# A graph network's message stage: from the scheduler's order to one fixed order of half-quad steps

## The chip, the cores and the metric

The kernel runs on one core of a Trainium2 chip. The metric is device time in microseconds (us). Before the change the median of 3 runs is 2623.31 us (2615.97 to 2633.4).

Engines are named as in the profile: PE (matrix multiply; PEld is its weight load), DVE (vector), ACT (activation), POOL (here almost only the issue of gathers), SP (here the issue of plain DMAs). L734 is line 734 of the kernel before the change.

## What is computed

A graph of 3125 nodes with 96 features and 100000 edges, sorted by destination, goes through four residual blocks: a ten-hop propagation, a softmax-weighted aggregation (layer 1), an edge-conditioned message block, and two graph convolutions. Each block gets the layer-normalised, rectified features. The change concerns the third block, whose core in the reference is:

```python
def _mlp(h, W, b, gamma, beta):
    h = jax.nn.relu(h @ W + b)
    mu = jnp.mean(h, axis=0)
    var = jnp.mean(jnp.square(h - mu), axis=0)
    return gamma * (h - mu) * jax.lax.rsqrt(var + EPS) + beta
node_feat = _mlp(x, W_node, b_node, g_node, beta_node)
edge_feat = _mlp(edge_attr, W_edge, b_edge, g_edge, beta_edge)
row, col = (edge_index[0], edge_index[1])
message = jnp.concatenate([x[row], x[col], edge_feat], axis=1)
message = _mlp(message, W_msg, b_msg, g_msg, beta_msg)
agg = jax.ops.segment_sum(message, col, num_segments=node_feat.shape[0])
return agg + node_feat
```

`row` is the source of an edge, `col` its destination.

## The kernel before

The kernel is written tile by tile in a framework that tracks the data dependencies, sets all semaphores, gives out buffers from pools (`bufs=n` buffers of one name in rotation), and orders the instructions of each engine by a planner of its own. So the program text of a loop is not the order in which an engine gets its instructions. Each engine then works strictly through its list.

Edges and nodes are first turned into count matrices (the first 400 us or so); ten hops of matrix products follow (`gather`, L372 to L384), then layer 1 (L574 to L654), which walks over 25 blocks of 128 nodes. For each block, layer 1 also writes two tables to DRAM: `Pt` (the source part of the message product) and `Qt` (the destination part), as pairs of fp16 halves, high and low (L637 to L644). Pools opened by then: `up` with two large fp16 tiles `u`, `mid`, and `late` (L532), whose tiles live until the end.

The message stage (L658 to L778) takes the edges in 98 quads of 1024 edges; a quad has two halves of 4 x 128 edges. The destinations of a quad lie within 128 consecutive nodes from the quad's first destination on. At its head the stage fetches three index lists from DRAM (`rlT`, `srow`, `rows`, L661 to L666) and builds a comparison pattern `li` on POOL (L667, L668). Then, for each quad:

- SP reads the quad's first node from `rows` into a register (L712) and loads `qg` (128 rows of `Qt`, L715), `et` (edge attributes, three buffers, L720) and `rlb` (destinations relative to the first, spread over 128 partitions, L722; four buffers in the space of `h`).
- DVE turns the destinations into two one-hot matrices: `ohT` (L724) and `oh` (L726).

and for each half:

- POOL gathers the source rows of `Pt`, one indirect DMA for each 128 edges, four in all (L733 to L735), into one of six buffers `pgs` that lie in a `u` tile.
- PE multiplies the edge attributes (`ef`, L737); ACT rectifies them to fp16 `eh` (L739), DVE takes the remainder `el` (L741).
- PE sums four products for each 128 edges into `pre` (PSUM, two buffers): with `ohT` and `qg` (L745), with `eh` (L746), with `el` (L747), and the gathered rows through the identity (L748).
- ACT copies the low part (`mt`, L750), DVE adds the high part (L751) and takes the maximum with 0 less the estimate `cb` of the mean (`m`, L753). ACT and DVE split `m` into an fp16 pair (L761, by L369 and L370) in one of four buffers `mms`, which also lie in a `u` tile and are listed in the profile as `u`.
- PE adds the pair to the quad's sums by `oh` (`segs`, L766) and to the Gram matrix (`gram`, L768).

At the end of a quad, PE adds what the last quad had for this quad's first node (`carry`, L765); ACT and DVE make `sacc` from `segs` (L771, L772), and SP stores it to `Sd` (L773). From the fifth quad on one of 15 pieces of the node branch is done per quad (`node_piece`, L687 to L708; its PSUM tile shares the two `ef` buffers). In the last half DVE clears the 352 edges that do not exist (L759).

After the stage `gs` is read from `gram` (L778), five small weights are loaded (L781 to L783), and the last two layers begin with the load of `Sd` (L793) and two tiles `u` from the pool `l3` (L790).

Of the kernel before, what the change touches and what calls it, by code (L numbers as in the profile page):

```python
# [9 lines left out]
F32 = mybir.dt.float32  # L10
F16 = mybir.dt.float16
I32 = mybir.dt.int32
F8 = mybir.dt.float8e4
U8 = mybir.dt.uint8
AF = mybir.ActivationFunctionType
ALU = mybir.AluOpType
# [4 lines left out]
P = 128  # L21
N, D, E = 3125, 96, 100000
NB = 25
NP = NB * P
EP, EC = 125, 800
GC = 8
# [3 lines left out]
HC = 4  # L30
# [10 lines left out]
Q, QE = 98, 1024  # L41
# [13 lines left out]
def narrow(ctx: ExitStack, tc: tile.TileContext, a: dict, out: bass.AP, flag: bass.AP):  # L55


    nc = tc.nc
# [33 lines left out]
    where = [const]  # L92
# [252 lines left out]
    def over_b(t, nb=NB):  # L345

        return t[:, None, :].to_broadcast([P, nb, D])
# [19 lines left out]
    def split(hi, lo, t):  # L367

        S.activation(hi, t, AF.Copy)  # L369
        V.tensor_sub(lo, t, hi)  # L370
# [200 lines left out]
    V.memset(hT[0][D:, :], 1.0)  # L571
    cb = where[-1].tile([P, D], F32, name="cb")

    with tc.tile_pool(name="l1", bufs=1) as lp, tc.tile_pool(name="l1w", bufs=3) as wp, \  # L574
            tc.tile_pool(name="l1p", bufs=3, space=PSUM) as pp, tc.tile_pool(name="l1q", bufs=1, space=PSUM) as qp:
        ps = qp.tile([P, 2, D], F32, name="pq")
# [81 lines left out]
    with tc.tile_pool(name="msg", bufs=1) as lp, tc.tile_pool(name="gath", bufs=6) as gp, \  # L658
            tc.tile_pool(name="msgw", bufs=3) as wp, tc.tile_pool(name="msgs", bufs=1, space=PSUM) as p1, \
            tc.tile_pool(name="msgp", bufs=2, space=PSUM) as p2:  # L660
        rlT = lp.tile([P, Q * 8], F16, name="rlT2")  # L661
        nc.sync.dma_start(rlT, rlT_d)
        srow = lp.tile([P, Q * 8], I32, name="srow")
        nc.sync.dma_start(srow, srcT_d)
        rows = lp.tile([1, Q], I32, name="rows")
        nc.sync.dma_start(rows, row_d)  # L666
        li = lp.tile([P, P, 4], F16, name="li2")  # L667
        G.iota(li, pattern=[[1, P], [0, 4]], base=0, channel_multiplier=0, allow_small_or_imprecise_dtypes=True)  # L668

        t = up.tile([P, NB, 2 * D + 2], F16, name="u").rearrange("p b d -> p (b d)")  # L670
        mms = [t[:, i * HC * GM:(i + 1) * HC * GM].rearrange("p (c d) -> p c d", c=HC) for i in range(4)]
# [35 lines left out]
                    T.transpose(ps[:, s, :], rT[:, c0 + s * P:c0 + (s + 1) * P], ident[:D, :D])  # L707
                V.tensor_add(x[:, b0:b0 + nb, :], x[:, b0:b0 + nb, :], ps)  # L708

        acc = None  # L710
        for g in range(Q):
            r0 = nc.values_load(rows[0:1, g:g + 1], engines=(mybir.EngineType.SP,), min_val=0, max_val=N - 1,  # L712
                                skip_runtime_bounds_check_because="a dst is a node")
            qg = gp.tile([P, 2 * D], F16, name="qg")
            nc.sync.dma_start(qg, Qt[bass.ds(r0, P), :])  # L715
            et = wp.tile([18, QE], F16, name="et")
            n = min(QE, E - g * QE)
            if n < QE:
                V.memset(et, 0.0)
            nc.sync.dma_start(et[:, :n], ea_d[:, g * QE:g * QE + n])  # L720
            rlb = rlbs[g % len(rlbs)]
            nc.sync.dma_start(rlb, bass.AP(tensor=rl_d.tensor, offset=rl_d.offset + g * QE, ap=[[0, P], [1, QE]]))  # L722
            ohT = wp.tile([P, QE], F16, name="ohT")
            V.tensor_scalar(ohT, rlb, part, None, ALU.is_equal)  # L724
            oh = wp.tile([P, 2, P, 4], F16, name="oh")
            V.tensor_tensor(oh, li[:, None, :, :].to_broadcast([P, 2, P, 4]),  # L726
                            rlT[:, g * 8:g * 8 + 8].rearrange("p (s c) -> p s c", s=2)[:, :, None, :].to_broadcast(
                                [P, 2, P, 4]), ALU.is_equal)
            seg = segs[:, g % 2, :GM]
            for half in range(GC // HC):  # L730
                k0 = g * GC + half * HC
                pg = pgs[(g * (GC // HC) + half) % len(pgs)]
                for c in range(HC):  # L733
                    G.indirect_dma_start(out=pg[:, c, :], out_offset=None, in_=Pt,  # L734
                                         in_offset=bass.IndirectOffsetOnAxis(ap=srow[:, k0 + c:k0 + c + 1], axis=0))  # L735
                ps = p2.tile([P, 512], F32, name="ef")[:D, :]
                T.matmul(ps, We, et[:, half * HC * P:(half + 1) * HC * P], start=True, stop=True)  # L737
                eh = wp.tile([D, HC * P], F16, name="eh")
                S.activation(eh, ps, AF.Relu)  # L739
                el = wp.tile([D, HC * P], F16, name="el")  # L740
                V.scalar_tensor_tensor(el, ps, 0.0, eh, ALU.max, ALU.subtract)  # L741
                ps = p2.tile([P, HC, 256], F32, name="pre")[:, :, :2 * D]
                for c in range(HC):
                    cs = slice(c * P, (c + 1) * P)
                    T.matmul(ps[:, c, :], ohT[:, half * HC * P + c * P:half * HC * P + (c + 1) * P], qg, start=True, stop=False)  # L745
                    T.matmul(ps[:, c, :], eh[:, cs], W3h, start=False, stop=False)  # L746
                    T.matmul(ps[:, c, :D], el[:, cs], W3h[:, :D], start=False, stop=False)  # L747
                    T.matmul(ps[:, c, :], ident16, pg[:, c, :], start=False, stop=True)  # L748
                t = wp.tile([P, HC, D], F32, name="mt")
                S.activation(t, ps[:, :, D:], AF.Copy)  # L750
                V.tensor_add(t, t, ps[:, :, :D])  # L751
                m = wp.tile([P, HC, D], F32, name="m")
                V.scalar_tensor_tensor(m, t, 0.0, over_b(cb, HC), ALU.max, ALU.subtract)  # L753
                for c in range(HC):
                    first = E - (k0 + c) * P
                    for p0, pn in ((0, 32), (32, 32), (64, 64)) if first < P else ():
                        assert first <= p0 or first >= p0 + pn
                        if first <= p0:
                            V.memset(m[p0:p0 + pn, c, :], 0.0)  # L759
                mm = mms[(g * (GC // HC) + half) % len(mms)]  # L760
                split(mm[:, :, :D], mm[:, :, D + 2:], m)  # L761
                for c in range(HC):
                    last = half == GC // HC - 1 and c == HC - 1
                    if last and acc is not None:
                        T.matmul(seg[0:1, :D], carry[:, g:g + 1], acc, start=False, stop=False)  # L765
                    T.matmul(seg, oh[:, half, :, c], mm[:, c, :], start=half == 0 and c == 0, stop=last)  # L766

                    T.matmul(gram, mm[:, c, :D + 1], mm[:, c, :], start=g == 0 and half == 0 and c == 0,  # L768
                             stop=g == Q - 1 and last)
            new = wp.tile([P, D], F32, name="sacc")  # L770
            S.activation(new, seg[:, D + 2:], AF.Copy)  # L771
            V.tensor_add(new, new, seg[:, :D])  # L772
            nc.sync.dma_start(Sd[bass.ds(r0, P), :], new)  # L773
            acc = new
            if g >= 4:
                node_piece(g - 4)
        gs = where[-1].tile([D + 1, GM], F32, name="gs")
        V.tensor_copy(gs, gram)  # L778

# [4 lines left out]
    with tc.tile_pool(name="l3", bufs=1) as lp, tc.tile_pool(name="l3w", bufs=3) as wp, \  # L784
# [2 lines left out]
        V.tensor_scalar(dv, cnt_dst, 1.0, None, ALU.add)  # L787
        V.tensor_copy(dv, rsqrt(dv, "rs_dv"))
        us = [lp.tile([P, NB, D], F32, name=f"us{i}") for i in range(2)]
        u = [lp.tile([P, NB, 2 * D], F16, name=f"u3{i}") for i in range(2)]  # L790
        sd = lp.tile([P, NB, D], F32, name="sd")
        for b in range(0, NB, 5):
            nc.sync.dma_start(sd[:, b:b + 5, :], Sd[b * P:(b + 5) * P].rearrange("(b p) d -> p b d", p=P))  # L793
# [657 lines left out]
```

## Time and profile before

| what | us |
|---|---|
| runs | 2633.40, 2623.31, 2615.97 (median 2623.31) |
| the profiled execution's own time | 2632.28 |
| its span, first to last instruction | 2630.4 |
| last write of `Pt` issued (L644) | 1247.89 |
| `srow` fetched, issue (L664) | 1250.47 |
| first gather starts (L734) | 1254.04 |
| last gather starts | 2435.94 |
| last `sacc` done (L772) | 2461.63 |

The profile shows one execution. A row of a group of instructions gives line, engine, operation, output and input, and count; then busy time and the mean duration of one in ns; then how long the engine stood idle just before these instructions, and what ended most of that. "issue" is an idle time without a visible releaser, and "remote" one whose releaser is unknown. In the tables of windows the columns are: window, length, busy time (and count) of PE, PEld, DVE, ACT and POOL, granted clock of PE as a share of full speed, share of the DMA engines, GB/s. In a timeline each line has start, duration, engine, line, operation, tiles, count, and in brackets the idle time before and its releaser. The chain of waits lists start, duration and the work that the end of the program hung on.

### The profile page before, as it was taken

Reading aid. Unit: us, or ns where it says so; the run is one execution under the profiler, and the core shown is the slowest. Engines: PE = TensorE matmul, PEld = TensorE weight load, DVE = VectorE, ACT = ScalarE, POOL = GpSimd, SP = SyncE. Lnnn points to the kernel's source line nnn. Section 1 sums busy time; section 2 is a strip of 40 time slices with the busy share of each in tenths; the row PEclk is TensorE's granted clock in tenths of the full one; section 3 lists DMA queues with packets and bytes.
Section 4 is the critical chain, followed back from the end, with each engine's and each line's share of the span. In section 5 each row is a group of like instructions: output and inputs, shape, how many; then the busy total and the mean of one; then the engine's idle time right before and its main releaser. Section 6 shows DMA issues by size and latency. Waiting matters only on the chain.

```text
span 2630.4 us, 44038 instructions
## 1 busy us (share of the span) xinstructions
PE 1915.0 (73%) x16190; PEld 1490.9 (57%) x16190; DVE 1524.0 (58%) x4164; ACT 962.3 (37%) x2332; POOL 825.8 (31%) x808
## 2 busy tenths in 40 slices
PE   0477777899999999998365666666666666656599
PEld 0222335778888899986244444444454544445488
DVE  2777999875655654876254444444444444454753
ACT  0398856479433311432132222222222222222440
POOL 4000000000000000000666567666666666667000
PEclk9799999999999999999577677677767676777699
DMA  2100000000000000001222222222222222222100
GB/s 71 57 17 1 1 1 1 6 9 10 10 10 10 10 21 2 15 20 46 54 72 64 56 65 65 69 65 69 65 71 65 70 65 67 66 66 55 26 1 21
DMA packets 101316, 100.66 MB, mean 38 GB/s; under 512 B 66285, under 2 KB 73206, under 8 KB 101090
## 3 DMA queue, kind: packets, MB, share of 16 engines
q1 hardware_dynamic: 73754, 54.78, 7.5%
q0 software_dynamic: 25088, 38.59, 6.3%
q10 hardware_dynamic: 2248, 4.40, 0.6%
q8 instruction: 128, 2.10, 0.3%
q14 instruction: 98, 0.80, 0.1%
HBM read 83.46 MB, written 14.21 MB: 37 GB/s over the span
## 4 chain that ended last, share of the span: by engine, by line
PE 51%; ACT 11%; DVE 9%; issue 7%; another core or an unknown queue 6%; POOL 1%; DMA 0%; ACTq 0%; SPq 0%; DVEq 0%; POOLq 0%
PE hop L380 19%; PE segs L766 4%; PE gram L768 4%; PE ef L737 4%; PE pre L746 4%; PE pre L748 4%; PE pre L745 3%; ACT x L524 3%; PE pre L747 2%; ACT eh L739 2%; ACT u L369 2%; PE eps L513 1%; ACT A L437 1%; ACT mt L750 1%
## 5 line engine op out<-in xcount | busy, mean ns | idle before, releaser
L734 POOL DMA_INDIRECT u<-Pt,srow x784 | 784.3, 1000 | 401.3 <-issue 169.0
L380 PE MATMUL hop<-u,A 128*128 128x192 f16 (+1 forms) x6250 | 547.6, 246 | 3.2 <-DVE degs L474 1.4
L380 PEld LDWEIGHTS <-A 128*128 128x128 fp8e4 x6250 | 520.5, 97 | 48.8 <-issue 44.1
L746 PE MATMUL pre<-W3h,eh 96*128 96x192 f16 x784 | 241.8, 309 | 306.3 <-issue 182.5
L751 DVE TENSOR_TENSOR mt<-mt,pre 128x384 f32<-128x384 f32 x196 | 108.3, 553 | 446.2 <-ACT mt L750 290.5
L750 ACT ACTIVATE mt<-pre 128x384 f32<-128x384 f32 x196 | 96.2, 491 | 613.8 <-PE pre L747 173.8
L746 PEld LDWEIGHTS <-eh 96*128 96x128 f16 x784 | 93.0, 119 | 399.0 <-issue 224.9
L745 PE MATMUL pre<-qg,ohT 128*128 128x192 f16 x784 | 240.4, 307 | 98.0 <-issue 52.1
L269 PE MATMUL cps<-hk,hl 128*128 128x500 f16 x784 | 230.5, 413 | 56.3 <-DVE hl L227 36.5
L668 POOL IOTA li<- 128x512 f16 x1 | 1.2, 1185 | 835.1 <-DMA et<-ea_d 835.1
L748 PE MATMUL pre<-u,ident 128*128 128x192 f16 x784 | 226.9, 303 | 29.0 <-issue 22.7
L766 PE MATMUL segs<-u,oh 128*128 128x194 f16 x784 | 237.4, 336 | 13.2 <-DVE u L370 9.7
L227 DVE TENSOR_TENSOR hk<-ki,keyT 128x4000 f16<-128x4000 f16 x98 | 220.4, 2249 | 44.1 <-PE cps L269 27.7
L768 PE MATMUL gram<-u 128*97 128x194 f16 x784 | 234.3, 331 | 2.8 <-issue 2.8
L273 ACT ACTIVATE C<-cps 128x500 f32 x269 | 162.9, 606 | 92.1 <-PE cps L272 64.8
L747 PE MATMUL pre<-W3h,el 96*128 96x96 f16 x784 | 188.5, 247 | 10.0 <-issue 8.5
L269 PEld LDWEIGHTS <-hl 128*128 128x128 f16 x784 | 73.6, 119 | 166.3 <-DVE hl L227 76.7
L514 ACT ACTIVATE eps<-eps 96x512 f32<-96x512 f32 x196 | 106.3, 568 | 151.9 <-PE eps L513 143.4
L768 PEld LDWEIGHTS <-u 128*97 128x97 f16 x784 | 145.5, 186 | 13.2 <-issue 7.2
L515 DVE BATCH_NORM_STATS2 x<-eps 96x6 f32<-96x512 f32 x196 | 134.1, 687 | 30.8 <-ACT eps L514 28.2
L741 DVE SCALAR_TENSOR_TENSOR el<-ef,eh 96x512 f16<-96x512 f32 x196 | 133.5, 683 | 28.5 <-issue 11.5
L484 DVE SCALAR_TENSOR_TENSOR wt<-hop,sc,h 128x96 f32<-128x96 f32 x225 | 69.9, 311 | 136.8 <-PE hop L380 136.8
(308 smaller groups left out, 3212.3 us busy)
## 6 DMA issues: line engine op xcount, KB each, us to landing
h<-rl_d SPq DMA_DIRECT2D x98, 256.0 KB
u<-Pt,srow POOLq DMA_INDIRECT x784
qg<-Qt SPq DMA_DIRECT2D x98, 48.0 KB
Sd<-sacc SPq DMA_DIRECT2D x98, 48.0 KB
x<-ea_d SPq DMA_DIRECT2D x195, 18.0 KB
et<-ea_d SPq DMA_DIRECT2D x97, 36.0 KB
et<-in_edge_attr_T ACTq DMA_DIRECT2D x4, 390.6 KB
ea_d<-eh SPq DMA_DIRECT2D x8, 195.3 KB
```

The lines of the kernel that those rows point to most:

```text
L227: V.tensor_tensor(t, pat[:, None, :, :].to_broadcast([P, s, n, c]), val[:, q, :].rearrange("p (s c) -> p s c", s=s)[:, :, None, :].to_broa ...
L269: T.matmul(ps, hl[:, j // 4, :, j % 4], hk[:, j // 2, :, j % 2], start=j == js[0], stop=n == 0 and j == js[-1])
L273: S.activation(C8[:, :, bass.ds(column_of(g), WIN)], ps, AF.Copy)
L380: T.matmul(ps[:, i, :], table[:, k, c0 + (b0 + i) * P:c0 + (b0 + i + 1) * P], u[:, k, :], start=k == 0, stop=k == NB - 1)
L515: V.bn_stats(stats[:, i, :], ps)
L734: G.indirect_dma_start(out=pg[:, c, :], out_offset=None, in_=Pt, in_offset=bass.IndirectOffsetOnAxis(ap=srow[:, k0 + c:k0 + c + 1], axis=0))
L745: T.matmul(ps[:, c, :], ohT[:, half * HC * P + c * P:half * HC * P + (c + 1) * P], qg, start=True, stop=False)
L746: T.matmul(ps[:, c, :], eh[:, cs], W3h, start=False, stop=False)
L747: T.matmul(ps[:, c, :D], el[:, cs], W3h[:, :D], start=False, stop=False)
L748: T.matmul(ps[:, c, :], ident16, pg[:, c, :], start=False, stop=True)
L766: T.matmul(seg, oh[:, half, :, c], mm[:, c, :], start=half == 0 and c == 0, stop=last)
L768: T.matmul(gram, mm[:, c, :D + 1], mm[:, c, :], start=g == 0 and half == 0 and c == 0, stop=g == Q - 1 and last)
```

## The change

1. The three index lists and the pattern `li` are fetched and built before layer 1, into the pool `late`.
2. The loop over quads is taken apart into functions, which are called step by step of a half, in a block in which each engine keeps the order of the program text (`tc.manual_schedule()`).
3. The products of a half are summed two steps after its messages. Edge features are computed one step ahead, gathers are issued five halves ahead, and a quad's loads two quads ahead and more. Within `pre` the products with `eh` and `el` come ahead of the one with `ohT`. `et` has four buffers instead of three.
4. The tiles `u` of the last two layers come from the pool `up`.

```diff
+    rlT = where[-1].tile([P, Q * 8], F16, name="rlT2")
+    nc.sync.dma_start(rlT, rlT_d)
+    srow = where[-1].tile([P, Q * 8], I32, name="srow")
+    nc.sync.dma_start(srow, srcT_d)
+    rows = where[-1].tile([1, Q], I32, name="rows")
+    nc.sync.dma_start(rows, row_d)
+    li = where[-1].tile([P, P, 4], F16, name="li2")
+    G.iota(li, pattern=[[1, P], [0, 4]], base=0, channel_multiplier=0, allow_small_or_imprecise_dtypes=True)
+
     with tc.tile_pool(name="l1", bufs=1) as lp, tc.tile_pool(name="l1w", bufs=3) as wp, \
...
-        rlT = lp.tile([P, Q * 8], F16, name="rlT2")
-        nc.sync.dma_start(rlT, rlT_d)
...
-        acc = None
-        for g in range(Q):
...
+        NH, PER = Q * (GC // HC), GC // HC
+        quad, half_ = {}, {}
+        st = {"acc": None}
+
+        def load_quad(g):
             r0 = nc.values_load(rows[0:1, g:g + 1], engines=(mybir.EngineType.SP,), min_val=0, max_val=N - 1,
                                 skip_runtime_bounds_check_because="a dst is a node")
             qg = gp.tile([P, 2 * D], F16, name="qg")
             nc.sync.dma_start(qg, Qt[bass.ds(r0, P), :])
-            et = wp.tile([18, QE], F16, name="et")
+            et = wp.tile([18, QE], F16, name="et", bufs=4)
...
+        def gather_rows(i):
+            for c in range(HC):
+                k = i * HC + c
+                G.indirect_dma_start(out=pgs[i % len(pgs)][:, c, :], out_offset=None, in_=Pt,
+                                     in_offset=bass.IndirectOffsetOnAxis(ap=srow[:, k:k + 1], axis=0))
...
+        def messages(i):
+            r0, qg, et, rlb, ohT, oh = quad[i // PER]
+            eh, el = half_[i]
+            ps = p2.tile([P, HC, 256], F32, name="pre")[:, :, :2 * D]
+            for c in range(HC):
+                cs = slice(c * P, (c + 1) * P)
+                T.matmul(ps[:, c, :], eh[:, cs], W3h, start=True, stop=False)
+                T.matmul(ps[:, c, :D], el[:, cs], W3h[:, :D], start=False, stop=False)
+                T.matmul(ps[:, c, :], ohT[:, i % PER * HC * P + c * P:i % PER * HC * P + (c + 1) * P], qg, start=False, stop=False)
+                T.matmul(ps[:, c, :], ident16, pgs[i % len(pgs)][:, c, :], start=False, stop=True)
...
+        with tc.manual_schedule():
+            for g in range(3):
+                load_quad(g)
+            for i in range(5):
+                gather_rows(i)
+            rows_hot(0)
+            cols_hot(0)
+            edge_features(0)
+            for i in range(NH + 2):
+                if i + 1 < NH:
+                    edge_features(i + 1)
+                if i >= 2:
+                    summed(i - 2)
+                if i < NH:
+                    messages(i)
+                g = i // PER + 1
+                if i % PER == 0 and g < Q:
+                    rows_hot(g)
+                if i % PER == 1:
+                    if g < Q:
+                        cols_hot(g)
+                    if g + 2 < Q:
+                        load_quad(g + 2)
+                    if g > 4:
+                        node_piece(g - 5)
+                if i + 5 < NH:
+                    gather_rows(i + 5)
...
-        u = [lp.tile([P, NB, 2 * D], F16, name=f"u3{i}") for i in range(2)]
+        u = [up.tile([P, NB, 2 * D + 2], F16, name="u")[:, :, :2 * D] for i in range(2)]
```

The functions not shown hold the lines of the old loop unchanged: `rows_hot` L724, `cols_hot` L726, `edge_features` L736 to L741, the rest of `messages` L749 to L761, `summed` L762 to L774 (with `sacc` and its store at the second half of a quad).

## The prediction, made before the result was known

> **What bounds the kernel now.** I read the page first, then the stages in windows, then the message stage by its waits and its timeline. All times are us of the profiled execution: span 2630.4, its own time 2632.28, which is 8.97 over the median of the runs (2623.31). Differences are worked out on the trace and taken off the median.
>
> ```profile
> PE 1915.0 (73%) x16190; PEld 1490.9 (57%) x16190; DVE 1524.0 (58%) x4164; ACT 962.3 (37%) x2332; POOL 825.8 (31%) x808
> ...
> L734 POOL DMA_INDIRECT u<-Pt,srow x784 | 784.3, 1000 | 401.3 <-issue 169.0
> ...
> L746 PE MATMUL pre<-W3h,eh 96*128 96x192 f16 x784 | 241.8, 309 | 306.3 <-issue 182.5
> ...
> L750 ACT ACTIVATE mt<-pre 128x384 f32<-128x384 f32 x196 | 96.2, 491 | 613.8 <-PE pre L747 173.8
> ```
>
> The page's mean hides the stage: POOL is 31% of the span, but all its gathers (L734) lie between 1254.04 and 2435.94. The windows (PE, PEld, DVE, ACT, POOL busy, granted clock) show that no engine is full there:
>
> ```profile
> 1700.00:1900.00 200.00, 125.22 (x871) 93.82 (x870) 94.48 (x187) 52.92 (x119) 134.66 (x134) 0.72 0.26 67
> 1900.00:2100.00 200.00, 129.29 (x881) 95.82 (x880) 92.33 (x187) 51.25 (x119) 133.29 (x136) 0.72 0.27 67
> ```
>
> 136 gathers in 200 us are 17 quads, so a quad (8 gathers, 2 halves) takes 11.8. The timeline of POOL shows what a gather costs and where POOL stands still:
>
> ```profile
> 1992.00 0.94 POOL L734 DMA_INDIRECT u<-Pt,srow  x1 [0.30 <-remote]
> 1993.25 1.15 POOL L734 DMA_INDIRECT u<-Pt,srow  x1 [0.30 <-issue]
> 1994.70 0.94 POOL L734 DMA_INDIRECT u<-Pt,srow  x1 [0.30 <-issue]
> 1995.95 0.95 POOL L734 DMA_INDIRECT u<-Pt,srow  x1 [0.30 <-issue]
> 1997.21 0.95 POOL L734 DMA_INDIRECT u<-Pt,srow  x1 [0.30 <-issue]
> 1999.95 0.94 POOL L734 DMA_INDIRECT u<-Pt,srow  x1 [1.79 <-PE pre L748]
> ```
>
> Each gather has 0.30 of dead time ahead of it even when it waits for nothing, and once a quad POOL waits for PE (1.79) to free a gather buffer. The timeline at the same place shows why PE is late: it works from 1991.98 to about 1999.2, then nearly stands until 2003.78, while pre goes to ACT (mt), DVE (mt), and the next ef and eh come back. The chain of waits there:
>
> ```profile
> 1998.93 0.88 PE pre L748
> 1999.81 0.49 ACT mt L750
> ...
> 2000.32 0.56 DVE mt L751
> ...
> 2000.93 0.32 PE pre L745
> 2001.25 1.52 PE ef L737
> ...
> 2003.15 0.38 ACT eh L739
> ...
> 2004.14 0.49 ACT eh L739
> ...
> 2004.68 0.34 PE pre L746
> ```
>
> So the stage is a ring of hand-overs, run for two halves at a time, with POOL some 12% idle behind it.
>
> **The change, part by part.**
>
> *1. Order of the stage.* Nothing is computed anew: matmuls, ACT, DVE instructions and gathers keep number and shape; only order and lag change. In a step (one half) PE does ef for the next half, the sums of two halves ago, then the messages. I ask what each engine needs per step.
> - POOL: 4 gathers of 1.00 (row) + 0.30 (timeline) = 5.20.
> - PE: the timeline spaces 192-column matmuls by 0.16 and 96-column ones by 0.08 at clock 0.50, half that at 1.00. Messages 4 x (0.16+0.16+0.08+0.16) = 2.24, sums 8 x 0.16 = 1.29, ef 0.43, half a carry pair 0.25: 4.2 at the low clock, 2.1 at the high one.
> - DVE: mt 0.553, m 0.549, u 0.551, el 0.683, half of ohT 0.518, oh 0.689 and sacc 0.246: 3.06. ACT: eh 0.588, mt 0.491, u 0.519, half of sacc 0.248: 1.72.
>
> POOL is the largest even with PE at half clock. Two steps of lag and four mm buffers let PE do other work while ACT and DVE turn the last half; a gather for half i+5 needs only messages(i-1) finished, so POOL has five halves of lead. Gathers from first to last: 783 x 1.30 = 1018 against 1181.9 now: **-164**.
>
> The hand-over is hidden by the lag as long as it fits. Ring over two steps: delay L from the last matmul to ACT's mt, then 0.49+0.55+0.55+0.52+0.55 = 2.66 to the finished u, 1.55 sums and carry, 2.24 messages: L + 6.45. In the trace L was as long as 3.9 (the half whose last L748 starts at 2007.68 and whose mt starts at 2011.59), because both halves' matmuls are mixed and complete together; that gives (3.9+6.45)/2 = 5.2 a step, equal to POOL. In layer 1 the same hand-over (pq to hv at 1186.27) takes under 0.1. In fixed order I expect the short one.
>
> Bounds of the pace: the median interval of gathers that do not wait is 1.25, giving 979; upwards, gathers that overlap the DVE instruction m (L753; two SBUF inputs) last 1.168 on average, the others 0.952 (123 and 410 of them, 1500 to 2300), so +0.22. Should all six such DVE instructions of a quad (m, u, twice; oh; ohT) cost that, a quad takes 8 x 1.245 + 6 x 0.22 = 11.3, the stage 1105. I take 1.30: it is the mean with DVE already beside POOL for 88% of the time.
>
> The Trainium skill, "SBUF — State Buffer", section "Who interferes with whom", speaks against the change: DVE with two SBUF inputs and a GpSimd instruction that reads SBUF exclude each other, and the later one stands until the first has ended. By it the six instructions would add up to 3.4 to a quad, an estimate of 13.4 a quad and 1310 for the stage. The row (+0.22 beside m, of 0.55) shows a partial wait; here the row decides.
>
> *2. End of the stage.* Now the last gather starts at 2435.94 and the last sacc ends at 2461.63: 25.7, since PE is two quads behind. After: landing 2.5 (1255.77 to the L748 at 1258.30), matmul 0.35, mt and m with ACT 1.7, eight memsets 1.5 (L759), u 1.2, sums and carry 1.9, sacc 0.6 = 9.8. **-16**. If PE is still behind: 0.
>
> *3. Index lists.* srow's fetch starts at 1250.47 and the first gather at 1254.04. Without it the gather waits for the last Pt write, issued at 1247.89; the last Sd store took 1.6 from sacc's end to its release (2463.25), so 1249.5: **-4.5** (bounds 0 and -6). The three DMAs (about 0.4 of SP each) and the iota (1.19 of POOL) move into layer 1, where SP has nothing between 1105.7 and 1113.28 and POOL none at all; they stand behind the weight loads in SP's queue, so layer 1's first need is not delayed. If that cover is gone they cost 2.4. They hold SBUF longer, for which the later u tiles move to another pool: no instruction changes.
>
> *4. Edges.* Before, two ohT and their rl_d loads (1232.85 to 1238.2) got between layer 1's last DVE steps and cost about 1.9. In the block they should come later: **-1** (0 to -1.9). At the end the five small weight loads (SP, 2.2), now issued around 1103.4, may come after the last Sd store, ahead of sd; sd is needed at 2471.01 and issued from 2463.23 to 2466.5, so they are covered; without cover +2.2. The SP queue: loads of quad g+2 stand behind the store of Sd, which waits for sacc; they are due some four steps (20 us) later, so nobody waits. The node pieces (15, up to 1.3 of PE at low clock) eat PE's margin of 1.0 a step in 15 steps; the lead of five halves covers them.
>
> Sum: -164 - 16 - 4.5 - 1 = -185.5. Span 2445, median 2623.3 - 185.5 = **2438**.
>
> **The rivals.**
> - *A hand-over takes the place of the waits.* If a delay L of 5 remains between PE and ACT in the new order too (mt waits behind PE for up to 7.1, once for 23.7, in this stage), a step takes (5+6.45)/2 = 5.7, the stage 196 x 5.7 = 1122, gain 60+21: **2542**. For it: the 3.9 above. Against: layer 1's short hand-overs. It would become slower than before at steps of 6.13 (L 5.8).
> - *POOL becomes slower (the other side).* With gathers back to back, each of the six DVE instructions could hold a gather for its whole length: 2 x 0.55 + 2 x 0.55 + 0.69 + 0.52 = 3.4 on 9.96, 13.4 a quad, stage 1310: +128 - 21 = **2730**. It decides from 12.27 a quad, that is 0.38 lost per such instruction; now the mean gather of 1.00 against 0.945 unhindered is 0.44 a quad, 0.07 each. Against it also: from 1255.77 to 1300.08 35 intervals in a row averaged 1.27, though with little DVE work.
> - *The change doesn't do what it says.* PE's waits put down to "issue" before L746 (182.5) and L745 (52.1) have no visible releaser; if they are PE's own and recur in any order, the stage stays at 1182 and only the edges go: **2602**. Against: most of them end just when eh is ready (eh ends 2003.73, L746 starts 2003.78).
>
> **How the numbers follow.** Chances: forecast 0.64, hand-over 0.16, POOL slower 0.12, waits stay 0.08. About 1% is what a measurement of this kernel can tell from no change. Forecast and hand-over are faster by over 1%: 0.80; 2602 is within 1% (0.8%): 0.08; slower 0.12. The forecast's own range goes from pace 1.25 (979: 2399) to the 11.3 quad (1105: 2525); with the hand-over's 2542 the range 2395 to 2545 holds 0.80.
>
> **What would show it.** Step 1: L734's idle near 235 (784 x 0.30) instead of 401, hardly any gather behind PE, gathers spanning about 1018, a quad about 10.4. Step 2: sacc ends about 10 after the last gather starts. Step 3: the first gather some 2 after the last Pt write is issued, and not after srow. Wrong if a quad is at 11 or more: then POOL's mean above 1.15 says port, POOL waiting for PE says hand-over or PE's own waits.

## The result, and the profile after

The change made no difference: 2630.67 us after (median of 16 runs, 2620.46 to 2637.60) against 2629.12 before (16 runs, 15 of them from 2615.97 to 2636.39), a ratio of 1.0009 with a 95% interval of 0.9993 to 1.0024. I had forecast 2438. The sixteenth run before took 3528.4, and the ratio leaves it out as slow. The profiled execution of after has a span of 2621.6 and a time of 2623.51, 7.2 below its median, so the profiles are compared here by their stages, and the totals by the medians.

First the page of after (busy us, share, instructions; then groups with mean ns, and the idle time before them):

```profile
PE 1975.0 (75%) x16190; PEld 1516.1 (58%) x16190; DVE 1540.0 (59%) x4164; ACT 959.6 (37%) x2332; POOL 819.6 (31%) x808
...
L736 POOL DMA_INDIRECT u<-Pt,srow x784 | 778.0, 992 | 550.8 <-issue 180.2
...
L792 PE MATMUL segs<-u,oh 128*128 128x194 f16 x784 | 225.8, 323 | 232.7 <-DVE ohT L741 139.4
...
L771 ACT ACTIVATE mt<-pre 128x384 f32<-128x384 f32 x196 | 96.1, 490 | 605.9 <-PE pre L769 249.6
...
L766 PE MATMUL pre<-W3h,eh 96*128 96x192 f16 x784 | 259.0, 330 | 15.4 <-issue 14.6
```

A gather costs 0.992 (1.000 before). POOL's idle time of 550.8 holds one wait of 153.6, for the first gather; the rest is 397.2 against 401.3 before, where I expected 235. The 306.3 that PE stood ahead of L746 are gone (15.4 at L766), but 232.7 now stand ahead of the first sum, L792. The windows of the stage (PE, PEld, DVE, ACT, POOL busy, granted clock, DMA share, GB/s) show the same pace, 135 to 136 gathers in 200 us:

```profile
1800.00:2000.00 200.00, 141.31 (x876) 103.07 (x875) 97.30 (x187) 53.34 (x119) 133.81 (x136) 0.62 0.29 68
2000.00:2200.00 200.00, 140.90 (x880) 102.43 (x878) 96.62 (x187) 53.35 (x119) 132.97 (x135) 0.63 0.29 67
```

So the pace is that of before: from 1500 to 2200 a quad takes 11.9 (470 gathers; 466 before). PE's granted clock is lower than before (0.62 in these windows against the 0.72 shown with the prediction), but it does not set the pace: "few loads" below has 159 gathers in 200 us at 0.71 on one chip and 138 at 0.69 on another. One half in the timeline (start, duration, and the idle time before it with what ended it):

```profile
1805.00 0.24 DVE L798 TENSOR_TENSOR sacc<-sacc,segs 128x96 f32<-128x96 f32 x1
...
1805.29 0.32 PE L792 MATMUL segs<-u,oh 128*128 128x194 f16 x1 [2.31 <-DVE ohT L741]
...
1808.61 0.37 PE L769 MATMUL pre<-u,ident 128*128 128x192 f16 x1
...
1810.26 0.94 POOL L736 DMA_INDIRECT u<-Pt,srow  x1 [0.30 <-issue]
...
1812.07 0.32 PE L766 MATMUL pre<-W3h,eh 96*128 96x192 f16 x1
...
1812.77 0.24 PE L767 MATMUL pre<-W3h,el 96*128 96x96 f16 x1 [0.38 <-issue]
...
1813.10 0.94 POOL L736 DMA_INDIRECT u<-Pt,srow  x1 [1.90 <-PE pre L769]
1813.11 0.49 ACT L771 ACTIVATE mt<-pre 128x384 f32<-128x384 f32 x1 [4.81 <-PE pre L769]
```

The last message matmul of a half ends at 1808.98 by the record. ACT, which waits for nothing else, starts mt at 1813.11, 4.1 later; POOL, waiting for the same matmuls, goes on at 1813.10. The trace also holds the times at which PE's semaphore counted up, which I call its signals (20 a quad in either order). Between 1795 and 1818 they came at:

```
1800.24 to 1801.24 (10)   1801.86   1802.59   1803.31 to 1803.40 (3)   1804.82 1804.85   1805.54 to 1805.60 (3)
none for 7.17
1812.77 to 1813.12 (10)   1813.71   1814.46   1815.17 to 1815.25 (3)   1816.68 to 1816.77 (3)   1817.44 1817.48
```

Ten signals within 0.35 cannot be ten groups of matmuls done in that time (matmuls of 192 columns start 0.16 apart here): by the record they had been done, and their signals were held. The end of a matmul is modelled in the profile, so this alone does not tell late signals from late matmuls. Over the whole stage mt starts 3.72 after the recorded end of its half's last matmul (mean of 196). The hold shown begins as POOL gathers back to back and ends once POOL stands still, waiting for PE.

The experiments fell on five chips, and the kernel before took 2450.5 (one run) on one of them (A), against 2608 to 2622 on the others (B, C, D, E), so each run is read only beside the run of before from its own chip.

### The profile page after: what moved, and what is told of

It is laid out like the page before. It is cut to its first block, busy times and chain, and to the rows that moved or that the text cites. A ratio compares the mean times of both kernels' runs of the same rounds, so it can differ in the third digit from the quotient of the medians.

```text
span 2621.6 us, 43748 instructions
## 1 busy us (share of the span) xinstructions
PE 1975.0 (75%) x16190; PEld 1516.1 (58%) x16190; DVE 1540.0 (59%) x4164; ACT 959.6 (37%) x2332; POOL 819.6 (31%) x808
## 4 chain that ended last, share of the span: by engine, by line
PE 44%; DVE 16%; issue 13%; ACT 9%; another core or an unknown queue 1%; DMA 0%; SPq 0%; DVEq 0%; ACTq 0%; POOL 0%; POOLq 0%
PE hop L380 19%; PE segs L792 4%; PE gram L794 3%; PE pre L769 3%; PE pre L768 3%; ACT x L524 3%; DVE u L370 3%; PE pre L766 3%; DVE mt L772 2%; DVE m L774 2%; PE ef L753 2%; ACT mt L771 2%; PE pre L767 1%; PE eps L513 1%; ACT A L437 1%
## 5 line engine op out<-in xcount | busy, mean ns | idle before, releaser
L736 POOL DMA_INDIRECT u<-Pt,srow x784 | 778.0, 992 | 550.8 <-issue 180.2
L792 PE MATMUL segs<-u,oh 128*128 128x194 f16 x784 | 225.8, 323 | 232.7 <-DVE ohT L741 139.4
L768 PE MATMUL pre<-qg,ohT 128*128 128x192 f16 x784 | 256.9, 328 | 25.6 <-issue 25.3
L769 PE MATMUL pre<-u,ident 128*128 128x192 f16 x784 | 258.5, 330 | 22.4 <-issue 21.4
L269 PE MATMUL cps<-hk,hl 128*128 128x500 f16 x784 | 232.7, 418 | 54.1 <-DVE hl L227 35.5
L794 PEld LDWEIGHTS <-u 128*97 128x97 f16 x784 | 137.2, 175 | 235.2 <-issue 231.5
L766 PE MATMUL pre<-W3h,eh 96*128 96x192 f16 x784 | 259.0, 330 | 15.4 <-issue 14.6
L767 PE MATMUL pre<-W3h,el 96*128 96x96 f16 x784 | 204.8, 261 | 28.5 <-issue 25.5
L369 ACT ACTIVATE u<-m 128x384 f16<-128x384 f32 x196 | 102.5, 523 | 243.5 <-DVE m L774 204.2
L370 DVE TENSOR_TENSOR u<-m,u 128x384 f16<-128x384 f32 x196 | 109.5, 559 | 115.6 <-issue 86.7
L792 PEld LDWEIGHTS <-oh 128*128 128x128 f16 x784 | 101.5, 129 | 109.4 <-issue 109.4
```

The costliest lines, as they stand in the source:

```text
L269: T.matmul(ps, hl[:, j // 4, :, j % 4], hk[:, j // 2, :, j % 2], start=j == js[0], stop=n == 0 and j == js[-1])
L736: G.indirect_dma_start(out=pgs[i % len(pgs)][:, c, :], out_offset=None, in_=Pt, in_offset=bass.IndirectOffsetOnAxis(ap=srow[:, k:k + 1], a ...
L766: T.matmul(ps[:, c, :], eh[:, cs], W3h, start=True, stop=False)
L768: T.matmul(ps[:, c, :], ohT[:, i % PER * HC * P + c * P:i % PER * HC * P + (c + 1) * P], qg, start=False, stop=False)
L769: T.matmul(ps[:, c, :], ident16, pgs[i % len(pgs)][:, c, :], start=False, stop=True)
L794: T.matmul(gram, mm[:, c, :D + 1], mm[:, c, :], start=i == 0 and c == 0, stop=g == Q - 1 and last)
```

## Experiments on chip A: what bounds the stage

Before took 2450.5 beside these four, one run each.

**Few gathers.**

```diff
-                if i + 5 < NH:
+                if i + 5 < 6:
                     gather_rows(i + 5)
```

> Leaves out all gathers after the first six halves (24 of 784 stay); the messages read old rows. Theory A (the gathers hold up PE: in the trace after, PE's signals to ACT and POOL arrive 3 to 7 us after the recorded matmuls, once a quad none arrives for 7.2 us): the hold goes, a quad falls from 11.9 to the 9.3 that PE's recorded matmuls take, or less, the stage to 910 or less, the whole to about 2360. Theory B (PE's real work takes all of 11.9 and the records only run ahead of it): nothing changes, 2600 to 2630. Theory C (the new order's own ring sum, sacc, next sum is the bound, with nothing held): 11 to 11.9 a quad, 2540 to 2630.

**Rows unread.**

```diff
-                G.indirect_dma_start(out=pgs[i % len(pgs)][:, c, :], out_offset=None, in_=Pt,
+                G.indirect_dma_start(out=pgs[i if i < 3 else 3 + i % 3][:, c, :], out_offset=None, in_=Pt,
...
-                T.matmul(ps[:, c, :], ident16, pgs[i % len(pgs)][:, c, :], start=False, stop=True)
+                T.matmul(ps[:, c, :], ident16, pgs[i % 3][:, c, :], start=False, stop=True)
```

> All 784 gathers run, but into three tiles that nobody reads; the messages read three tiles gathered at the start (so the output is not the reference's). PE no longer waits for a gather, POOL no longer for PE. Theory A in the form that the traffic of the gathers or POOL's work on them holds up PE: the stage stays at 1130 or above, the whole over 2580. Theory A in the form that PE's waits on the gathers' signals are what costs: as without gathers, a stage of about 1020 (POOL alone, 784 x 1.25 to 1.30) or what PE then needs, the whole 2440 to 2470. Theory B: 2600 to 2630.

**Few loads of target numbers.**

```diff
-            rlb = rlbs[g % len(rlbs)]
-            nc.sync.dma_start(rlb, ...)
+            rlb = rlbs[g % 3]
+            if g < 3:
+                nc.sync.dma_start(rlb, ...)
```

> Leaves out the 256 KB load of each quad's target numbers after the third quad (95 of 98); the one-hot rows are made from old numbers. If this load is what PE's signals wait behind (they come at 0.2 bursts a us while the hardware queue moves data, at 0.8 while it doesn't): the 7.2 us hold shrinks by the load's 2 to 3 us, the stage to 900 to 950, the whole about 2390. If it is not: within 1% of after, 2605 to 2655.

**No gram.**

```diff
-                T.matmul(gram, mm[:, c, :D + 1], mm[:, c, :], start=i == 0 and c == 0, stop=g == Q - 1 and last)
+                if i < 2 or i >= NH - 2:
+                    T.matmul(gram, mm[:, c, :D + 1], mm[:, c, :], start=i == 0 and c == 0, stop=g == Q - 1 and last)
```

> Leaves out the matmuls of the second sum (gram) in all but the first and last two halves: 768 of 784, a sixth of PE's columns in the stage. Theory B (PE's work is the bound): 1.3 a quad less, the stage 125 shorter, the whole near 2505. Theory A (PE is held up, not busy): less than 30 shorter, 2600 to 2630.

Measured: few gathers 2163.4, rows unread 2432.1, few loads 2417.2, no gram 2441.4. None of the expectations fitted. For the last three that is because before itself was 2450.5 here; the 2360 that I expected without gathers was too high on either kind of chip (2173.8 on C, below), since a quad without gathers takes 6.85 (mean of the middle 60) and not the 9.3 that I took from PE's records. What the four share is that nothing is held. The timeline of "no gram" at the end of a half:

```profile
1808.67 0.37 PE L769 MATMUL pre<-u,ident 128*128 128x192 f16 x1
1808.89 0.94 POOL L736 DMA_INDIRECT u<-Pt,srow  x1 [0.31 <-PE pre L768]
1809.07 0.49 ACT L771 ACTIVATE mt<-pre 128x384 f32<-128x384 f32 x1 [1.28 <-PE pre L769]
```

mt starts 0.03 after the matmul's recorded end (mean of 196: 0.05), beside a running gather. And a window of the same run:

```profile
1800.00:2000.00 200.00, 158.40 (x855) 102.42 (x853) 111.82 (x213) 60.58 (x136) 152.45 (x157) 0.50 0.32 79
```

157 gathers in 200, a quad of 10.2 with PE at clock 0.50 (10.3 over the stage); its gathers span 1010.9, and the last sacc ends 11.4 after the last gather starts. That is what the forecast's first two steps said (10.4, 1018, 9.8), here with a sixth of PE's columns left out. "Few loads", which keeps all of PE's work, comes to the same: its gathers span 990.5, the last sacc ends 11.6 after the last gather starts, and mt starts 0.06 after its matmuls. Its window here, and below it that of the same kernel on chip C, which follows later:

```profile
1800.00:2000.00 200.00, 155.54 (x1036) 109.17 (x1036) 116.44 (x219) 61.63 (x139) 151.75 (x159) 0.71 0.21 54
...
1800.00:2000.00 200.00, 126.72 (x893) 93.55 (x891) 96.25 (x187) 53.47 (x119) 137.88 (x138) 0.69 0.19 46
```

The same program, nearly the same clock: 159 gathers in 200 on A, 138 on C. But the old order seems to need no rescue on A: from 2450.5 less the 1254 ahead of the stage, about 168 behind it and a tail of 11 to 26, it has 1000 to 1015 left for its gathers, an estimate, since no trace of before was kept there. Without gathers the whole is 2163: POOL is worth 250 to 280 there.

## The change, and a part of it, on other chips

> The changed kernel as it is, because the kernel before took 2450.5 beside the first four experiments and 2629 in the runs shown so far, and because none of those four traces has PE's signals arriving in steps of 0.7 us. Theory S (the steps come from where or when a program runs, and hide what the order does): where before takes about 2450, after is bound by POOL at 10.3 a quad, the stage 1010 to 1020, the whole 2430 to 2445, 0.3 to 1% faster than before; where before takes about 2630, after takes 2620 to 2640 again. Theory A (the gathers hold up PE wherever it runs): a stage of 1180 and about 2630 in any case. The prediction's sum, if before is 2450 only because it has no holds: 2265, which POOL's 10.3 a quad excludes.

> The kernel before, for its trace beside the run above. Theory S: no steps of 0.7 us between PE's signals; if the whole is near 2450, a quad takes 10.3 to 10.6 with POOL waiting for hardly anything, so that the old order too is bound by POOL. Theory A: 11.8 a quad and the steps, about 2630.

**Lists only:** the kernel before, with only the second part of the change.

```diff
+    srow = where[-1].tile([P, Q * 8], I32, name="srow")
+    nc.sync.dma_start(srow, srcT_d)
...
-        srow = lp.tile([P, Q * 8], I32, name="srow")
-        nc.sync.dma_start(srow, srcT_d)
...
-        u = [lp.tile([P, NB, 2 * D], F16, name=f"u3{i}") for i in range(2)]
+        u = [up.tile([P, NB, 2 * D + 2], F16, name="u")[:, :, :2 * D] for i in range(2)]
```

> Only the second part of the change: index lists and the iota in layer 1, the later u tiles in the other pool, the message stage's order as before. The prediction's step: the first gather 4.5 earlier, 0 to 6, so 2 to 6 below before. Rival: the first gather only moves ahead of other work that sets the end anyway, 0.

> The changed kernel a third time. The job of the first four experiments ran on another chip than the jobs that showed before at 2616 and 2629; there before took 2450.5, and no PE signal came in 0.7 us steps. Theory S (the steps belong to the chip): if before is near 2450 here, after takes 2425 to 2445 (POOL-bound, 10.3 a quad, and the edges of the change some 10 to 20 less); if before is near 2620 here, after takes 0.995 to 1.001 of it, as twice already. Rival: the order itself costs or gains several per cent on one of the two kinds of chip.

> The changed kernel beside the two runs above, for the two by two table. Beside a before near 2620: 0.995 to 1.001 of it, as three times already. Beside a before near 2450: 0.99 to 1.0.

| chip | before, median | after / before, 95% interval | lists only / before |
|---|---|---|---|
| B | 2616.4 | 0.9963 (0.9941 to 0.9985) | 0.9979 (0.9962 to 0.9995) |
| C | 2616.1 | 0.9969 (0.9952 to 0.9986) | |
| E | 2621.7 | 0.9996 (0.9978 to 1.0013) | |

The trace of before on B (2626.7 in that run) has the same stage as the one on record: 11.9 a quad, gathers from first to last 1173.1 (1181.9 on record). After has 1160.8, 1173.8 and 1176.1 on B, C and E (1174.2 on record). So the whole change takes 7.7 off the gathers' span on record and 12.3 on B, where "lists only", in the old order, takes 7.5 off (1165.6): next to nothing is left of the 164 that I had summed for the order. By the ratios on B the whole change gains 9.7 (3.9 to 15.4) and the lists alone 5.5 (1.3 to 9.9), inside the 2 to 6 expected; the two are not told apart. After took 2603.6 on B, below the 2620 to 2640 I expected, and 0.997 and 1.000 of before on C and E, as expected. This fits theory S, by which what hides the order goes with where a program runs. Each chip was used in one batch of runs alone, so the chip is not told apart from that batch. After itself never fell on a chip like A, so its gain there was not measured.

## What of a gather holds PE up

On C, beside a before of 2616.1, I ran three of the first kernels again.

> Leaves out all gathers after the first six halves, as the first experiment did, which took 2163 beside a before of 2450.5. Beside a before near 2620, the gathers' part in the steps shows: if the gathers or PE's waits for them cause the steps, they go, and the whole is 2160 to 2180 here too; if the steps are there without gathers, the stage keeps an idle PE, 2300 or more. Beside a before near 2450: 2163 again.

> All gathers run into tiles that nobody reads; the messages read rows gathered at the start, PE waits for no gather and gives 4 fewer signals a half. Beside a before near 2620: if the traffic of the gathers causes the steps, PE still shows them although it waits for nothing, and the messages end near POOL or after it, the whole 2450 to 2600; if PE's waits for gathers, or the number of its signals, cause them, no steps, 2432 as before. Beside a before near 2450: 2432 again.

> Leaves out the 256 KB load of target numbers after the third quad. Beside a before near 2620: if this load causes the long hold of each quad (7.2 us without a PE signal), the quad falls from 11.9 to 10.3 and the whole to 2420 to 2450; if the gathers alone do, the whole stays over 2560. Beside a before near 2450: 2417 again.

Measured: few gathers 2173.8, as on A; few loads 2615.6, as before; rows unread 3180.5, against 2432.1 on A. The load of target numbers is out, the gathers are it, and PE need not wait for a gather to suffer. "Few gathers" on C shows both conditions in one run. Its 24 gathers run back to back at the head of the stage; the third half's last matmul, the last gather, and that half's mt:

```profile
1266.27 0.32 PE L769 MATMUL pre<-u,ident 128*128 128x192 f16 x1
...
1279.51 0.94 POOL L736 DMA_INDIRECT u<-Pt,srow  x1 [0.30 <-DMA u<-Pt,srow]
...
1283.44 0.49 ACT L771 ACTIVATE mt<-pre 128x384 f32<-128x384 f32 x1 [17.03 <-remote]
```

No PE signal comes between 1263.71 and 1282.71, and mt starts 16.85 after its matmul, once the gathers are over; in the same place on A it starts 0.04 after. The timeline of "rows unread" on C:

```profile
1702.69 0.32 PE L769 MATMUL pre<-u,ident 128*128 128x192 f16 x1 [2.48 <-issue]
1702.99 1.09 POOL L736 DMA_INDIRECT u<-Pt,srow  x1 [0.30 <-issue]
1704.09 0.10 PEld L766 LDWEIGHTS <-eh 96*128 96x128 f16 x1 [2.70 <-issue]
1704.38 1.10 POOL L736 DMA_INDIRECT u<-Pt,srow  x1 [0.31 <-issue]
1705.49 0.32 PE L766 MATMUL pre<-W3h,eh 96*128 96x192 f16 x1 [2.48 <-issue]
1705.79 1.09 POOL L736 DMA_INDIRECT u<-Pt,srow  x1 [0.30 <-issue]
1706.89 0.10 PEld L767 LDWEIGHTS <-el 96*128 96x128 f16 x1 [2.70 <-issue]
```

In this stretch each PE instruction, load or matmul, begins 0.01 after a gather ends (1702.99 + 1.09 = 1704.08; 1704.09), and none during one: one instruction for 1.40 us. From 1500 to 2200 it is 498 instructions beside 500 gathers; half of them begin like this, the others mostly in short bursts, also during a gather. Its windows while POOL gathers, and when it is done, and below them one of the same kernel on A:

```profile
1800.00:2000.00 200.00, 20.57 (x72) 8.50 (x71) 10.30 (x18) 6.43 (x12) 153.54 (x144) 0.50 0.15 37
...
2600.00:2800.00 200.00, 150.66 (x1526) 119.33 (x1524) 161.78 (x323) 88.73 (x207) 0.00 (x0) 0.98 0.21 60
...
1500.00:1700.00 200.00, 146.95 (x1518) 116.29 (x1518) 163.80 (x325) 88.01 (x206) 155.51 (x147) 1.00 0.40 95
```

72 matmuls in 200 us with gathers on C, 1526 without; on A 1518 beside the same gathers. (The totals hide part of this: on A the messages were done at 1985, and the 2432 is the time of POOL's gathers, which end at 2281; on C the messages end at 3011.) In the real kernel, as I read it, it does not come to this because POOL must wait for PE, and PE's signals come out in those waits: in after (record, 1500 to 2200) POOL's pauses are 14% of the time and carry 43% of PE's signals, 5.1 a us against 1.1 a us outside them. A quad is then eight gathers of 1.25 to 1.3 and the pause of 1.6 that lets PE out, in the old order as in the new. One difference stays: in after 69% of PE's recorded starts lie within gathers, which fill 67% of the time, so its instructions, as recorded, do not avoid the gathers as those of "rows unread" do. Whether in after the instructions are late or only their signals is not shown.

On D, beside a before of 2608.4, four kernels asked what it is about a gather.

> Leaves out the second sum (gram) in all but four halves: 32 of the 104 instructions that PE has in a quad, none of its 20 signals. Beside a before near 2450 it took 2441, bound by POOL. Beside a before near 2620 (gathers hold up PE; with POOL running free PE began one instruction for each gather): if PE's instructions are what has to get through POOL's pauses, the 1.6 to 1.9 that POOL stands still in a quad shrink by a third, 11.9 to 11.3, the whole 2550 to 2570; if only its signals have to, the whole stays at 2590 to 2615.

**Plain copies by POOL** (and, in the next, by SP):

```diff
-                G.indirect_dma_start(out=pgs[i % len(pgs)][:, c, :], out_offset=None, in_=Pt,
-                                     in_offset=bass.IndirectOffsetOnAxis(ap=srow[:, k:k + 1], axis=0))
+                b = k % NB * P
+                G.dma_start(out=pgs[i % len(pgs)][:, c, :], in_=Pt[b:b + P])
```

> Each gather becomes a plain copy of 128 consecutive rows from the same table, issued by POOL into the same tile, with the same waits (other rows, so the output is not the reference's). Beside a before near 2620: if any transfer that POOL issues holds up PE, the stage stays over 1120 and the whole over 2560; if only indirect ones do, PE is free and the whole is 2160 to 2440, by what such a copy costs POOL. Beside a before near 2450: the same, without telling.

> The same plain copies from SP's queue: the same bytes and waits, POOL idle. If what holds up PE is the data moving, the steps stay and the whole is over 2500 beside a before near 2620; if it is POOL's work of issuing, they go: SP needs about 8 x 0.35 a quad, PE and DVE then bound the stage at 8 to 9.3 a quad, the whole 2170 to 2330.

**Iota for gather:** "rows unread" with this in place of each gather from the fourth half on.

```diff
+                    G.iota(pgs[3 + i % 3][:, 2 * (c % 2):2 * (c % 2) + 2, :], pattern=[[1, 2], [0, 2 * D]], base=0,
+                           channel_multiplier=0, allow_small_or_imprecise_dtypes=True)
```

> From the fourth half on, each gather becomes an iota of 128x384 on POOL into tiles that nobody reads (about 0.9 us, no transfer), POOL waiting for nobody; the messages read rows gathered at the start. To be held against the run with unread gathers (3180 beside a before of 2616): if POOL's being busy is enough to hold up PE, PE crawls again until POOL is done and the whole is over 2800; if it takes a transfer, PE runs free and the whole is 2163 to 2220.

Measured: no gram 2602.0, plain by POOL 2151.5, plain by SP 2156.4, iota 2466.6. So it is not the bytes (SP moved them), nor that POOL issues a transfer (784 plain copies of 0.538 each, in the same queue as the gathers, q0 software_dynamic, and mt 0.35 after its matmuls, as without gathers, 0.33 on A): what is left is the indirect gather. The copies read other rows, consecutive ones, and POOL paused 0.58 or 1.96 after every four of them (1600 to 1625), so copies without a pause were not tried. The group and a window of "plain by POOL":

```profile
L737 POOL DMA_DIRECT2D u<-Pt x784 | 416.9, 538 | 440.6 <-PE pre L769 289.6 <-DVE ln_r_t L115 135.2 <-PE pre L768 5.0
```

```profile
1600.00:1800.00 200.00, 151.47 (x1535) 119.96 (x1532) 161.84 (x323) 88.88 (x206) 124.62 (x236) 0.98 0.44 117
```

POOL moved 236 tiles in that window, far more than the 136 of after, and PE ran at clock 0.98. Nor do fewer PE instructions help: without gram 32 of some 100 a quad are gone, and a quad still takes 11.75 (477 gathers from 1500 to 2200), where after's takes 11.8 to 11.9 in its four traces. The iota run met another lock:

```profile
1268.87 309.44 DVE L745 TENSOR_SCALAR ohT<-h,part 128x1024 f16<-128x1024 f16 x1
```

```profile
L740 POOL IOTA u<- x772: 463/465/662, 1263.8 to 1577.4; 128x384 f16 x193
```

One DVE instruction of 0.5 us lasted 309.44, until the last of 772 iotas (1577.4 + 0.5) was done, and PE stood behind DVE. 2163 + 303 is the time, so the total answers nothing. But the first 6 us of its iotas, before DVE's stop is felt, do:

```profile
1269.54 0.37 PE L773 MATMUL pre<-u,ident 128*128 128x192 f16 x1
...
1269.94 0.49 ACT L775 ACTIVATE mt<-pre 128x384 f32<-128x384 f32 x1 [0.96 <-PE pre L773]
```

From 1263.81 POOL runs iotas without a gap. PE begins 70 instructions up to 1270.31, its signals come (1265.69, 1265.72, 1266.26, 1267.52, 1269.92), and mt starts 0.04 and 0.09 after its matmuls; just before, beside the gathers, one mt came 2.15 late. In so short a stretch, that POOL is busy does not hold PE.

**Fewer signals, in either order**, on E beside a before of 2621.7. With the instructions ruled out, I took the signals to be what has to get through POOL's pauses, and moved the gathered rows from PE to DVE, so that PE neither waits for a gather nor releases one; the kernel before got the same edit.

```diff
-                T.matmul(ps[:, c, :], ident16, pgs[i % len(pgs)][:, c, :], start=False, stop=True)
+            pg = pgs[i % len(pgs)]
+            m = wp.tile([P, HC, D], F32, name="m")
+            V.tensor_add(m, pg[:, :, :D], pg[:, :, D:])
...
             V.tensor_add(t, t, ps[:, :, :D])
+            V.tensor_add(t, t, m)
```

> The changed order, with the gathered rows added by DVE instead of PE: 8 matmuls of 104 instructions less a quad, and PE gives 5 signals a quad instead of 20, since it no longer waits for a gather nor releases one (DVE does); DVE has 4 instructions of 0.55 more a quad, 8.4 in all. Theory of the signals (what has to get through POOL's pauses is PE's signals): beside a before near 2620 a quad falls from 11.9 to between 10.2 and 11.1 (POOL's 8 x 1.27, plus up to 0.22 for each of four more DVE instructions of two SBUF inputs), the whole 2440 to 2540. Rival (PE is held up whatever it signals, DVE's longer turn adds to the ring): 11.9 or more, 2610 to 2720. Beside a before near 2450 (no hold): 2440 to 2530, by DVE's contention alone.

> The order before, with the same move of the gathered rows from PE to DVE: about 6 signals a quad instead of 20. Theory of the signals: beside a before near 2620 it falls too, to 2460 to 2560, and the new order with it is 10 to 40 faster than this (the end of the stage, 16, and the lists, 4.5, of the prediction's steps). If the new order is needed to use the freed PE: 2580 or more, and the gain is in the order. Rival as above: 2610 to 2720.

Measured: 2790.4 in the new order (1.0638, 1.0564 to 1.0712) and 2748.5 in the old (1.0481, 1.0443 to 1.0519). That theory falls: 5 to 6 signals a quad instead of 20, and a quad takes 13.6 and 13.1. POOL's longest kind of wait in the new order (in total, times, longest):

```profile
POOL u L736 <- DVE m L771: 314.7, 57, 10.8
```

POOL no longer waits for PE at every half but mostly runs 16 gathers (four halves) back to back, and then stands for 5.5 on average (314.7 / 57). Outside its pauses PE gets 0.22 signals a us through, and mt starts 5.3 after its matmuls (1500 to 2200; 3.6 in after). My reading is that what counts is not how many signals there are but how often POOL lets go. It is not shown: DVE's longer turn, the rival put on record with these runs, would lengthen a quad too, and no run parts the two. Neither of these two versions beats the two kernels.

## Why the prediction was wrong

- **The step that failed** is in part 1: "In layer 1 the same hand-over (pq to hv at 1186.27) takes under 0.1. In fixed order I expect the short one." The delay L of 3.9 was taken for a result of the mixed order. It is there in the fixed order too: 3.72 on average on the record's chip, against 0.05 and 0.06 on A (no gram, few loads). Layer 1 has no gathers beside it, so its hand-over was the wrong row; the right one was the 3.9 itself. The length of L is not all: by the prediction's own ring 3.72 still gives (3.72 + 6.45) / 2 = 5.1 a step. The sum also let POOL and PE run independently of each other, and in after POOL's gathers hold up PE's signals and POOL then waits for them, 1.6 a quad on top of its eight gathers.
- **Part 1's pace** of 5.20 a step is what POOL does where nothing is held: 10.3 a quad on A. There, though, the old order cannot be far from it either (1000 to 1015, by the estimate above), so the 164 seems to be in neither kind of chip: on one it is not lost before, on the other this order did not bring it.
- **A wait I did not see**: the first sum of a quad waits for DVE's sacc of the quad before (1805.24, then L792 at 1805.29), though it writes the other half of `segs`. In 79 of 97 quads the first sum starts within 0.09 of that sacc's end, and PE has stood 194 in all ahead of these (in "no gram" on A it is 5 quads and 4.3). It puts DVE's turn behind every hold. No run took this wait away, so what it costs on a held chip is open.
- **Part 2** (end of stage, -16): its condition "If PE is still behind: 0" came true, 27.7 against 25.7 on record; unheld it is 11.4, near the 9.8.
- **Part 3** (lists, -4.5): right in its mechanism. The first gather starts 2.5 after the last Pt write is issued (1249.96 to 1252.44; 6.15 before); alone it was worth 0.9979.
- **Part 4**: no cover was lost; the time from the last sacc to the end is 167.2 against 168.8. The -1 at the end of layer 1 does not show: the last Pt write is issued at 1249.96 against 1247.89, in one execution each.
- **The rivals**: the port's was wrong (the mean gather is 0.992, not over 1.15), and of its six instructions ohT (L724) reads one tile, not two; the hand-over's formula was too kind, since it let nothing else wait. "The change doesn't do what it says" came as to the stage's pace, without the gain of its 2602, and I gave it 0.08, because PE's waits end as eh becomes ready. That was a circle: eh, too, comes behind a PE signal (in before ACT stands 2.33 ahead of the mt at 2002.76, waiting for PE; eh follows it at 2003.15).

What stays open: why chips B to E hold PE up and A does not, which path of the chip a gather and PE's instructions share, and whether it would be so without the profiler, since every run here was profiled. That a chip keeps its kind was not tried, since none of the five came up in two batches.

## What to carry to other kernels

Compare the recorded end of a matmul with the start of the instruction that waits for nothing else: a delay of microseconds there is not the order's fault, and here neither of two orders took it away. Before a stage is reordered, take the suspected neighbour out (the gathers, on C: 2174) and let it run free with nobody waiting for it (on C: 3180, beside a before of 2616): these two runs showed what the bound is made of. And run the kernel before on several chips before a wait is read as a property of the program.

## What was not expected of the hardware

- While POOL runs indirect gathers back to back, PE on chip C begins about one instruction for each gather (498 beside 500, mostly 1.40 apart); on chip A the same kernel is not held (1518 matmuls in 200 us, 748 us less in all). The Trainium skill, "SBUF — State Buffer", section "Who interferes with whom", says that PE and ACT never wait on anyone for SBUF ports. Whether it is a port that PE waits for no run here shows; that it does wait beside POOL's gathers, the run of 3180 shows, and plain copies by POOL, with their pauses, did not do it.
- An f16 tensor_scalar on DVE stood for 309 us beside iotas on POOL that followed one another without a gap (0.41 apart). The same section says that a tensor_scalar can take the pair of ports that DVE shares with GpSimd, and that the later one then waits for the other's whole instruction; here DVE did not get in between some 750 instructions (309 / 0.41). That it was this port no run here shows. DVE's f32 instructions passed beside the first iotas (m in 0.56 at 1263.85).
- PE's signals come in steps where they are held: of the intervals over 0.1 between them, 227 of 453 are 0.65 to 0.80 in after (record, 1500 to 2200), and 19 of 1314 in the run without gram on A.
